# A graph-attention and slice-attention layer in float32: two orders of tokens for contiguous operands, two transposes moved to TensorE, denominators from a column of ones

## Chip, cores, metric

One core of a Trainium2 chip. The metric is the device time of one execution in microseconds (us), the median of several; all values quoted are of runs in the fast state. "Span" is the time from the first to the last record of the one profiled execution. A pass is one TensorE matmul instruction; a float32 matmul takes two (the views below have x32 for a run of 16 matmuls). The stationary operand of a matmul is the one that a weight load (LDWEIGHTS) puts in place, the moving operand is the other. In the views PE stands for the matmuls of TensorE, PEld for its weight loads, DVE for VectorE, ACT for ScalarE, POOL for GpSimd, SP for SyncE, and a `q` behind a name for the sequencer of that engine.

## The reference, cut to what matters

`x` is (32, 512, 256) float32: 32 batches of 512 tokens. Every batch goes through

```python
x = x + gnn(layernorm(x), adj, ...)     # mlp1 256->512, attention without mask, mlp2 512->256, attention with mask
x = x + ffn(layernorm(x), ...)          # softmax over 64 slices per head, sums per slice, attention among slices, back
# _gat: h = inp @ W; e = leaky_relu(f1_i + f2_j); att = softmax(e, axis=2); elu(att @ h)
# ffn:  w = softmax((x @ W_x @ W_slice) / temp); tok = (w^T x) W_fx / sum(w); attention; out = w @ out_slice
```

Each product needs one operand with features on the partitions and the other with tokens there, so every batch has several transposes.

## The kernel before

The kernel records all operations of the 32 batches and lets a list scheduler of its own merge them, so that three to four batches are in flight. The turns of the steps, a period and shifts for the first and last batches (`TURNS`, `PERIOD`, `HEAD`, `TAIL`) are constants found by a search and steer the order. Partition `p` of a tile of tokens holds tokens `4p..4p+3` (`NT` is 4), so a block of 128 tokens for one matmul is every fourth column of a feature-major tile:

```python
def every(cols, t):
    return cols[:, t::NT]
...
# h: the stationary operand (second argument) is strided
nc.tensor.matmul(pm, every(o0T[:, k], t), wfc[:, k, s, :], ...)
...
# transposes of the middle batches: VectorE turns 32x32 blocks, the DMA puts the blocks in place
def flip(src, dst):
    nc.vector.transpose(dst, src.rearrange("p (c i) -> p c i", i=Q))        # Q = 32
FLIPPED = ("xn", "u", "e", "o2", "w", "xn2", "s1")
flip(e, stage[:, :, i::NT]); ...; gather("e", stage, pT)     # 4 DMA writes to DRAM, 1 DMA back
...
# tokens: 16 small matmuls, 64 columns of stationary operand, s = 0 and 1 in the two halves of the array
for p in range(NP):
    for k in range(KD):
        for s in range(2):
            nc.tensor.matmul(pm[ts(s, C), p, :], wfx[:, k, ts(2 * p + s, C)],
                             every(s1T[:, k], p)[:, ts(s, G)], start=(p == 0 and k == 0), stop=False)
```

Of the kernel before, what the change touches and what calls it, by code (L numbers as in the profile page):

```python
# [15 lines left out]
TURNS = {  # L16
    "load": -28.1, "norm1": 42.5, "mlp1": 51.4, "h": 105.5, "factors": 105.5, "p": 114.2,
    "pv": 115.4, "o1": 126.5, "mlp2": 169.7, "h2": 183.7, "e": 190.4, "p2": 190.4,
    "pv2": 203.8, "norm2": 210.0, "w": 285.7, "sums": 288.2, "s1T": 298.5, "tokens": 342.3,
    "att": 351.0, "vo": 351.0, "gg": 361.3, "out": 377.9,  # L20
}
PERIOD, SPARE = 91.4, 0.00

HEAD, TAIL = (-48.2, -40.6, -1.9), (-3.9, 8.3, 26.1)


SAMPLE, SETUP = 8, 15.0

FLIPPED = ("xn", "u", "e", "o2", "w", "xn2", "s1")

P = 128
# [4 lines left out]
class Recorder:  # L36
# [4 lines left out]
    DRAIN = 0.17  # L41
    ISSUE, BEGIN, LAND, BEHIND = 0.45, 1.2, 0.9, 3.0
    KEPT = 1
# [62 lines left out]
    def _cost(self, op, out, ins):  # L106
# [6 lines left out]
        if op.method == "dma_start":  # L113
            side = next(ap for ap in (out, *ins) if ap.space != bass.MemoryType.DRAM)
            op.moving = out.size() * 4 / (250e3 if side.ap[0][1] <= P // 4 else 320e3)
            return self.ISSUE, 0.0
# [175 lines left out]
def adj_ffn_kernel(  # L292
# [71 lines left out]
    def gather(what, stage, dst):  # L364


        blocks, width = stage.shape[1:]
        scr = dram.tile([blocks, Q, P // Q, width], F32, name="scr", tag=f"scr_{what}", bufs=2)
        for a in range(P // Q):
            nc.sync.dma_start(  # L370
                scr[:, :, a, :].rearrange("c r j -> r c j"), stage[ts(a, Q), :, :]
            )
        nc.sync.dma_start(
            dst, scr.rearrange("(k c) r a j -> (c r) k (a j)", c=P // Q)
        )

    def every(cols, t):

        return cols[:, t::NT]

# [98 lines left out]
    adjt = new("adjt", [P, NT, N], tag="wT", dtype=I32)  # L479
    nc.sync.dma_start(adjt, adj.rearrange("(p t) j -> p t j", p=P))  # L480
    for t in range(NT):
        nc.vector.tensor_scalar(
            mbias[:, t, :].rearrange("p (t q) -> p t q", t=NT),
            adjt[:, t, :].rearrange("p (q t) -> p t q", t=NT), 0.0, None, op0=OP.is_gt,
        )
        nc.vector.tensor_scalar(
            mbias[:, t, :], mbias[:, t, :], -1.0, -MASKED, op0=OP.add, op1=OP.mult
        )
# [91 lines left out]

    def transpose_features(what, b, src, dst):

        if by_dma(what, b):
            stage = new(what + "_stage", [P, D // Q, P], tag="stage4")
            for t in range(NT):
                flip(src[:, t, :D], stage[:, :, t::NT])
            gather(what, stage, dst)
            return
        for k in range(KD):
            pt = tr_tile([P, N])  # L590
            for t in range(NT):
                nc.tensor.transpose(pt[:, ts(t)], src[:, t, ts(k)], ident)
            nc.scalar.copy(
                dst[:, k, :].rearrange("p (q t) -> p t q", t=NT),
                pt.rearrange("p (t q) -> p t q", t=NT),
            )

# [12 lines left out]
    def front(b):  # L610
# [7 lines left out]
        xnT = new("xnT", [P, KD, N])  # L618
        transpose_features("xn", b, xn, xnT)
        nc.step = "mlp1"  # L620
# [12 lines left out]
        for t in range(NT):  # L633
            for s in range(2):
                pm = mm_tile([P, HH + 1])
                for k in range(KH):
                    nc.tensor.matmul(
                        pm, every(o0T[:, k], t), wfc[:, k, s, :],
                        start=(k == 0), stop=(k == KH - 1),
                    )  # L640
                nc.scalar.copy(h[:, t, s, :], pm)
# [47 lines left out]
        for i in range(NT):  # L689
# [11 lines left out]
            if by_dma("u", b):  # L701
                flip(u, stage[:, :, i::NT])
                continue
            pt = tr_tile([P, KH, P])
            for m in range(KH):
                nc.tensor.transpose(pt[:, m, :], u[:, ts(m)], ident)
            nc.vector.tensor_tensor(o1T[:, :, i::NT], pt, o0T[:, :, i::NT], op=OP.add)
        nc.step = "o1"
        if by_dma("u", b):
            gather("u", stage, o1T)  # L710
            for m in range(KH):
                nc.vector.tensor_tensor(o1T[:, m, :], o1T[:, m, :], o0T[:, m, :], op=OP.add)
        return o1T

    def middle(b, o1T):
# [3 lines left out]
        for m in range(KD):  # L719
            pm = mm_tile([P, N])  # L720
            for k in range(KH):
                nc.tensor.matmul(
                    pm, w2[:, k, ts(m)], o1T[:, k, :], start=(k == 0), stop=(k == KH - 1)
                )
# [3 lines left out]
        for t in range(NT):  # L728
            pm = mm_tile([P, D + 2])
            for k in range(KD):  # L730
                nc.tensor.matmul(
                    pm, every(o2T[:, k], t), wh[:, k, :], start=(k == 0), stop=(k == KD - 1)
                )
# [8 lines left out]
        if by_dma("e", b):  # L742
            stage = new("e_stage", [P, N // Q, P], tag="stage")
        den = small("den", [P, NT])
        nmax = small("nmax", [P, NT])
        for i in range(NT):
# [7 lines left out]
            )  # L754
            nc.scalar.activation(
                e, e, AF.Exp, bias=nmax[:, i : i + 1], accum_out=den[:, i : i + 1]
            )
            if by_dma("e", b):
                flip(e, stage[:, :, i::NT])
                continue  # L760
            pt = tr_tile([P, NT, P])
            for j in range(NT):
                nc.tensor.transpose(pt[:, j, :], e[:, ts(j)], ident)
            nc.scalar.copy(pT[:, :, i::NT], pt)
        nc.step = "p2"
        if by_dma("e", b):
            gather("e", stage, pT)
        rd = small("rd2", [P, NT])
        nc.vector.reciprocal(rd, den)

        r2 = new("r2", [P, NT, D])
        if by_dma("o2", b):
            stage = new("o2_stage", [P, N // Q, KD * Q], tag="stage4")
            for k in range(KD):
                nc.vector.transpose(
                    stage[:, :, ts(k, Q)].rearrange("p (t c) i -> p t c i", t=NT),
                    o2T[:, k, :].rearrange("p (c i t) -> p t c i", t=NT, i=Q),
                )
            gather("o2", stage, r2)
        else:  # L780
            for t in range(NT):
                pt = tr_tile([P, D])
                for k in range(KD):
                    nc.tensor.transpose(pt[:, ts(k)], every(o2T[:, k], t), ident)
                nc.scalar.copy(
                    r2[:, t, :].rearrange("p (a k i) -> p k a i", k=KD, i=Q),
                    pt.rearrange("p (k a i) -> p k a i", k=KD, i=Q),
                )

# [3 lines left out]
        for i2 in range(NT // 2):  # L793
            pm = mm_tile([P, 2, D])
            for s in range(2):
                i = 2 * i2 + s
                for j in range(NT):
                    nc.tensor.matmul(
                        pm[:, s, :], every(pT[:, j], i), h[:, j, :D],
                        start=(j == 0), stop=(j == NT - 1),  # L800
                    )
            u, m = row("u2", (P, 2, D), "u"), row("m2", (P, 2, D), "m")
            elu_elu(
                [(pm[:, s, :], rd[:, 2 * i2 + s : 2 * i2 + s + 1], s) for s in range(2)], m, u
            )
            for s in range(2):
# [8 lines left out]
    def back(b, x1):  # L815
# [5 lines left out]
        xnT = new("xn2T", [P, KD, N])  # L821
        transpose_features("xn2", b, xn, xnT)

# [3 lines left out]
        if by_dma("w", b):  # L827
            stage = new("w_stage", [P, INNER // Q, P], tag="stage")
        for t in range(NT):
            pm = mm_tile([P, INNER])  # L830
            for k in range(KD):
                nc.tensor.matmul(
                    pm, every(xnT[:, k], t), weff[:, k, :], start=(k == 0), stop=(k == KD - 1)
                )
# [15 lines left out]
            if by_dma("w", b):  # L850
                flip(wt, stage[:, :, t::NT])
                continue
            pt = tr_tile([P, NP, P])
            for p in range(NP):
                nc.tensor.transpose(pt[:, p, :], w[:, t, ts(p)], ident)
            nc.scalar.copy(wT[:, :, t::NT], pt)
        if by_dma("w", b):
            gather("w", stage, wT)

# [5 lines left out]
        for p in range(NP):  # L865
# [9 lines left out]
            if by_dma("s1", b):  # L875
                flip(s1[:, p, :D], stage[:, :, p::NP])
        nc.step = "s1T"
# [3 lines left out]
        else:  # L881
            for k in range(KD):
                pt = tr_tile([P, INNER])
                for p in range(NP):
                    nc.tensor.transpose(pt[:, ts(p)], s1[:, p, ts(k)], ident)
                nc.scalar.copy(
                    s1T[:, k, :].rearrange("p (q n) -> p n q", n=NP),
                    pt.rearrange("p (n q) -> p n q", n=NP),
                )
# [13 lines left out]
        for p in range(NP):  # L903
            for k in range(KD):
                for s in range(2):
                    nc.tensor.matmul(
                        pm[ts(s, C), p, :], wfx[:, k, ts(2 * p + s, C)],
                        every(s1T[:, k], p)[:, ts(s, G)],
                        start=(p == 0 and k == 0), stop=False,
# [62 lines left out]
        for t2 in range(NT // 2):  # L972
            po = mm_tile([P, 2, D])
            for s in range(2):
                t = 2 * t2 + s
                for p in range(NP):
                    nc.tensor.matmul(
                        po[:, s, :], every(wT[:, p], t), gg[:, p, :],
                        start=(p == 0), stop=(p == NP - 1),
# [66 lines left out]
```

## Time and profile before

| | before |
|---|---|
| time, median | 2926 us |
| span of the profiled run | 2918.5 us |
| TensorE / VectorE / ScalarE busy | 97% / 76% / 36% |
| mean granted TensorE clock | 0.991 |
| first mm<-o1T,w of the 6th and of the 26th batch | 507.0, 2263.3 us |

The last row splits the run in three: filling up to the 6th batch (507 us), twenty steady batches (1756 us, 87.8 each) and emptying (655 us). In the views quoted below, a group's line is engine, operation, out<-in, shape and count; then busy time and mean ns of one; then the engine's idle time just before and what ended it. A timeline's line begins with start and duration in us.

### The profile page before, as it was taken

Reading aid. Unit: us, or ns where it says so; the run is one execution under the profiler, and the core shown is the slowest. Engines: PE = TensorE matmul, PEld = TensorE weight load, DVE = VectorE, ACT = ScalarE, POOL = GpSimd, SP = SyncE. Lnnn points to the kernel's source line nnn. Section 1 sums busy time; section 2 is a strip of 40 time slices with the busy share of each in tenths; the row PEclk is TensorE's granted clock in tenths of the full one; section 3 lists DMA queues with packets and bytes.
Section 4 is the critical chain, followed back from the end, with each engine's and each line's share of the span. In section 5 each row is a group of like instructions: output and inputs, shape, how many; then the busy total and the mean of one; then the engine's idle time right before and its main releaser. Section 6 shows DMA issues by size and latency. Waiting matters only on the chain.

```text
span 2918.5 us, 34260 instructions
## 1 busy us (share of the span) xinstructions
PE 2827.3 (97%) x11981; PEld 2301.0 (79%) x11981; DVE 2231.4 (76%) x4994; ACT 1042.8 (36%) x2058; POOL 125.2 (4%) x233
## 2 busy tenths in 40 slices
PE   8999899999999999999999999999999999999998
PEld 6787668887778887878887878887878877777776
DVE  6567768877778877778877778877778877788774
ACT  3533323333333333333333333333333333333232
POOL 0000000000000000000000000000000000000000
PEclk9999999999999999999999999999999999999998
DMA  5125345454445454445444445444445444444420
GB/s 163 31 72 143 96 128 152 129 147 131 134 139 151 127 148 129 135 135 157 123 145 130 137 137 156 126 144 130 138 137 153 129 140 129 136 138 116 137 73 15
DMA packets 459365, 373.24 MB, mean 128 GB/s; under 512 B 82229, under 2 KB 376761, under 8 KB 459065
## 3 DMA queue, kind: packets, MB, share of 16 engines
q1 hardware_dynamic: 455856, 368.92, 43.8%
q10 hardware_dynamic: 3336, 2.14, 0.2%
q8 instruction: 95, 1.56, 0.2%
q14 instruction: 78, 0.63, 0.1%
HBM read 196.91 MB, written 174.06 MB: 127 GB/s over the span
## 4 chain that ended last, share of the span: by engine, by line
PE 61%; DVE 21%; DMA 11%; SPq 3%; issue 2%; ACT 1%; DVEq 0%; ACTq 0%
PE mm L255 58%; DMA scr<-e_stage 5%; DVE e_stage L255 4%; SPq L255 3%; DMA o1T<-scr 3%; DVE e L255 3%; DVE w L255 3%; DVE w_stage L255 2%; PE tr L255 2%; DVE rs L255 2%; DVE nmax L255 2%; DMA scr<-u_stage 1%; PE sm L255 1%; DVE u L255 1%; DVE mx L255 1%
## 5 line engine op out<-in xcount | busy, mean ns | idle before, releaser
L255 PEld LDWEIGHTS mm<-wfc,o0T 128*128 128x128 f32 x2048 | 491.4, 327 | 19.3 <-PE tr L255 5.5
L255 PE MATMUL mm<-wfc,o0T 128*128 128x257 f32 x2048 | 498.7, 398 | 0.0
L255 PE MATMUL mm<-h,pT 128*128 128x256 f32 (+1 forms) x2048 | 486.8, 379 | 0.0
L255 PEld LDWEIGHTS mm<-h,pT 128*128 128x128 f32 x2048 | 390.2, 191 | 51.9 <-issue 2.8
L255 PE MATMUL mm<-xn,w 128*128 128x257 f32 x1024 | 272.8, 392 | 37.7 <-DVE fm L255 17.4
L255 PE MATMUL mm<-h,p2T 128*128 128x256 f32 x1024 | 301.3, 400 | 0.4 <-DMA p2T<-scr 0.4
L255 PEld LDWEIGHTS mm<-h,p2T 128*128 128x128 f32 x1024 | 266.7, 321 | 9.9 <-DMA p2T<-scr 0.7
L255 PE MATMUL mm<-xnT,w 128*128 128x512 f32 x512 | 258.6, 614 | 3.6 <-ACT xnT L255 3.3
L255 PE MATMUL mm<-gg,wT 128*128 128x256 f32 x1024 | 260.3, 401 | 0.0
L255 PEld LDWEIGHTS mm<-gg,wT 128*128 128x128 f32 x1024 | 251.5, 329 | 11.1 <-ACT gg L255 0.2
L255 PEld LDWEIGHTS mm<-xn,w 128*128 128x128 f32 x1024 | 186.6, 194 | 84.2 <-issue 50.6
L255 PE MATMUL mm<-weff,xn2T 128*128 128x512 f32 x512 | 243.6, 608 | 0.1
L255 ACT COPY h<-mm 128x257 f32<-128x257 f32 (+1 forms) x384 | 141.6, 369 | 279.6 <-PE mm L255 274.8
L255 PE MATMUL mm<-o1T,w 128*128 128x512 f32 x512 | 230.0, 602 | 9.6 <-DVE o1T L255 9.6
L255 DVE TENSOR_TENSOR o1T<-o1T,o0T 128x512 f32<-128x512 f32 x120 | 75.2, 687 | 157.6 <-DMA o1T<-scr 157.6
L255 PEld LDWEIGHTS mm<-o1T,w 128*128 128x128 f32 x512 | 96.0, 191 | 124.7 <-issue 91.6
L255 DVE SCALAR_TENSOR_TENSOR e<-f2b,h,mbias 128x512 f32<-128x512 f32 x128 | 92.4, 743 | 131.0 <-ACT f2b L255 129.0
L255 ACT ACTIVATE u<-mm,rd 128x256 f32<-128x256 f32 x192 | 90.0, 471 | 266.0 <-PE mm L255 159.1
L255 PEld LDWEIGHTS mm<-weff,xn2T 128*128 128x128 f32 x512 | 151.8, 315 | 40.2 <-ACT xn2T L255 1.3
L255 ACT ACTIVATE m<-m 128x512 f32<-128x512 f32 x192 | 118.0, 626 | 154.6 <-DVE m L255 154.1
L255 ACT ACTIVATE e<-e,nmax 128x512 f32<-128x512 f32 x128 | 92.4, 722 | 199.3 <-DVE nmax L255 199.3
L255 DVE STREAM_TRANSPOSE o_stage<-o2T 128x512 f32<-128x512 f32 x60 | 66.5, 1108 | 125.6 <-ACT o2T L255 123.9
(147 smaller groups left out, 4203.9 us busy)
## 6 DMA issues: line engine op xcount, KB each, us to landing
scr<-xn_stage SPq DMA_DIRECT2D x240, 128.0 KB, 2.6
scr<-u_stage SPq DMA_DIRECT2D x120, 256.0 KB, 4.5
o1T<-scr SPq DMA_DIRECT2D x30, 1024.0 KB, 6.1
scr<-e_stage SPq DMA_DIRECT2D x120, 256.0 KB, 4.9
p2T<-scr SPq DMA_DIRECT2D x30, 1024.0 KB, 5.6
scr<-w_stage SPq DMA_DIRECT2D x120, 256.0 KB, 4.1
wT<-scr SPq DMA_DIRECT2D x30, 1024.0 KB, 5.7
xt<-in_x_dram SPq DMA_DIRECT2D x32, 512.0 KB, 4.0
```

The lines of the kernel that those rows point to most:

```text
L255: getattr(getattr(self.nc, op.engine), op.method)(*op.args, **op.kwargs)
```

## The change

Intent: with `p = 32a+i`, let token `4p+t` stand at column `128a+32t+i` or at column `128t+p` in place of column `4p+t`, two orders in all, so that every stationary operand and every 32x32 transpose touches runs of 32 words or more; transpose the second layer norm (`xn2`) and the sums (`s1`) on TensorE; and get the softmax denominators of the second attention from a column of ones in `h2`. The scheduler's constants were searched anew; two costs in its model changed too, left out below (`BEHIND` 3.0 to 2.7, and the speed that it assumes for DMAs of 32 partitions, 250e3 to 215e3). The core of the diff, cut:

```diff
-TURNS = {"load": -28.1, "norm1": 42.5, ...}    PERIOD, SPARE = 91.4, 0.00
-HEAD, TAIL = (-48.2, -40.6, -1.9), (-3.9, 8.3, 26.1)
+TURNS = {"load": -84.2, "norm1": 231.3, ...}   PERIOD, SPARE = 94.3, 0.00
+HEAD, TAIL = (-18.3, -16.5, -8.8), (-4.0, -5.5, -4.1)
-FLIPPED = ("xn", "u", "e", "o2", "w", "xn2", "s1")
+FLIPPED = ("xn", "u", "e", "o2", "w")
-    def every(cols, t):
-        return cols[:, t::NT]
+    def swapped(cols):
+        return cols.rearrange("p (t a i) -> p a t i", t=NT, i=Q)
-                flip(e, stage[:, :, i::NT])                 # likewise xn, u, w
+                flip(e, stage[:, :, ts(i, Q)])
-                        pm, every(o0T[:, k], t), wfc[:, k, s, :],      # likewise o2T, p2T, wT, xn2T
+                        pm, o0T[:, k, ts(t)], wfc[:, k, s, :],
-            nc.scalar.activation(e, e, AF.Exp, bias=nmax[:, i : i + 1], accum_out=den[:, i : i + 1])
+            nc.scalar.activation(e, e, AF.Exp, bias=nmax[:, i : i + 1])
+        nc.vector.memset(h[:, :, D], 1.0)                   # and p2T @ h over D + 1 columns
+            raw = new("w_raw", [P, NP, N], tag="w")         # w comes back in the other order,
+            gather("w", stage_w, raw)                       # four ScalarE copies swap it into wT
-                        every(s1T[:, k], p)[:, ts(s, G)],   # moving operand of tokens
+                        s1T[:, k, :].rearrange("p (a n i) -> p n a i", n=NP, i=Q)[:, p, ts(s, 2)],
```

## The prediction

> **What bounds the kernel now.** I read the busy shares first, then the groups with shapes kept apart, then the timeline of TensorE in one steady batch, then the chain that ended last.
>
> ```profile
> PE 2827.3 (97%) x11981; PEld 2301.0 (79%) x11981; DVE 2231.4 (76%) x4994; ACT 1042.8 (36%) x2058; POOL 125.2 (4%) x233
> PE 61%; DVE 21%; DMA 11%; SPq 3%; issue 2%; ACT 1%; DVEq 0%; ACTq 0%
> ```
>
> TensorE is busy 97% of the span, so the time is what TensorE issues plus its waits. Successive batches start 87.6 us apart in the middle of the run (the first mm<-o1T,w of each batch); 32 x 87.6 = 2803, the rest of the 2918.5 us is filling and emptying the pipeline of batches. A matmul of float32 is two instructions (passes). Their mean durations overlap, so I take the pace from start times: gap to the next group over count.
>
> ```profile
> 1408.73 8.55 PE L255 MATMUL mm<-wfc,o0T 128*128 128x257 f32 x36
> 1417.11 0.67 PE L255 MATMUL mm<-xn,w 128*128 128x257 f32 x2
> ...
> 1443.35 10.55 PE L255 MATMUL mm<-h,pT 128*128 128x257 f32 x48
> 1453.74 0.27 PE L255 MATMUL sm<-ident,s 128*4 128x128 f32 x1
> 1453.94 2.07 PE L255 MATMUL mm<-s1T,wfx 128*64 128x64 f32 x32
> 1455.94 2.84 PE L255 MATMUL mm<-xnT,w 128*128 128x512 f32 x6
> ```
>
> A 257-column pass with a stationary operand taken at every fourth token costs (1417.11-1408.73)/36 = 233 ns; with one in one piece (1453.74-1443.35)/48 = 216.5 ns. The weight loads say why:
>
> ```profile
> L255 PEld LDWEIGHTS mm<-wfc,o0T 128*128 128x128 f32 x2048 | 491.4, 327 | 19.3 <-PE tr L255 5.5 <-issue 2.1
> L255 PEld LDWEIGHTS mm<-h,pT 128*128 128x128 f32 x2048 | 390.2, 191 | 51.9 <-issue 2.8 <-DVE pT L255 0.5
> ```
>
> 327 against 191 ns, most of it hidden under the running pass, so 136 ns more of load shows as only 16.5 ns. Under 512-column passes it is wholly hidden: ten strided mm<-weff,xn2T take 4.31 us, 431 ns each, and sixteen unstrided mm<-o1T,w 6.97 us, 436 each.
>
> **What the skill says.** (1) "SBUF — State Buffer", section "Door 1: The DMA port swizzle", has SBUF lines of 16 bytes with a penalty for each access in a new line. Four float32 are 16 bytes, the stride of this kernel, and the trace agrees: loads of 327 against 191 ns, and ScalarE copies out of PSUM of 1101 ns into a strided wT against 587 into f2b. (2) "TensorEngine Tiling (Array Packing)", "Key Properties": changing the tiling mode drains TensorE, and different tiles may load and multiply in parallel. The trace agrees on both: see the third part. (3) "VectorE: DVE Perf Modes", "The three transpose paths", tells only that VectorE transposes blocks of 32x32; the cost of a strided destination is not there. The trace has e_stage<-e at 1116 ns where other VectorE passes over 512 words take 660 to 690.
>
> **The change part by part.**
>
> *Strides.* Four groups of 256 to 258 columns get an unstrided stationary operand: wfc,o0T 2048 passes, h,p2T 1024, gg,wT 1024, wh,o2T 512; 4608 in all. 4608 x 16.5 ns = 76 us off TensorE. The 512 passes of weff,xn2T gain nothing.
>
> *Transposes onto TensorE.* In 30 batches 16 transposes are added (8 of xn2, 8 of s1); 16 of o2T at the two edge batches go: 464 more. Four tr<-ident,ex take 0.44 us, 110 ns each: 464 x 0.11 = +51 us on TensorE. In exchange VectorE loses 8 transposes of 0.64 us a batch, and the DMA queue two round trips.
>
> *Denominators.* h2 has a column of ones, so p2T passes have 257 columns instead of 256: under 1 us in all. ScalarE loses 128 accumulator reads (23.9 us), VectorE gets three small reciprocals and a memset a batch (0.5 us).
>
> *What only the order of the built kernel shows.* The tokens step (mm<-s1T,wfx, 64 columns of stationary, alternating between halves of the array) stood as one run of 16 matmuls in nearly every batch. In the changed kernel its 16 matmuls are strewn between mm<-h,pT: runs of 2, 4, 1, 1, 1, 1, 1, 1, 3, 1. Counted over the program, there are 263 such runs in place of 37. The filling phase of the kernel before happens to contain a few split runs:
>
> ```profile
> 394.42 0.70 PE L255 MATMUL mm<-h,pT 128*128 128x256 f32 x2
> 395.05 1.12 PE L255 MATMUL mm<-s1T,wfx 128*64 128x64 f32 x14
> 396.11 0.70 PE L255 MATMUL mm<-h,pT 128*128 128x256 f32 x2
> 396.74 1.12 PE L255 MATMUL mm<-s1T,wfx 128*64 128x64 f32 x14
> ...
> 2510.39 0.42 PE L255 MATMUL mm<-s1T,wfx 128*64 128x64 f32 x2
> 2510.74 0.65 PE L255 MATMUL mm<-nrow,bfx 4*64 4x256 f32 x4
> ```
>
> Two h,pT passes between two runs take 395.05-394.42 = 0.63 us instead of 0.43: +0.20 for going in (drain, about 0.09) and for the first full load after coming out, which nothing hides (about 0.10). A run of a single matmul takes 0.35 us by itself (2510.39 to 2510.74[...]), since its other half stands empty; an unbroken run of 16 takes 2.00 (1453.94 to 1455.94), 0.235 for each further pair. So a lone matmul costs 0.55 us. A steady batch: six lone ones 3.3; the 2 at 0.56; the 4 at 0.80; the 3 as two pairs 0.80; the last, which runs into nrow, 0.45; sum 5.9 us against 2.2 (2.00+0.20) before. That is +3.7 us a batch. Over the whole order, with the early and edge batches as they stand and a few nrow switches saved, I count +89 us.
>
> *Sum on TensorE:* -76 + 51 + 89 = **+64 us**. Added up instruction by instruction with these durations, the kernel before needs 2754 us, the changed one 2815: +61, which I use.
>
> *Waits.* The kernel before spends 2918 - 2754 = 164 us beyond that sum. The mean granted clock of 0.991 is 26 us of it, the start before the first matmul and the end after the last about 13, leaving some 125 for waits. About 1.5 us of each batch are waits of this kind:
>
> ```profile
> 1416.69 1.04 SPq L255
> 1417.77 4.65 DMA scr<-e_stage
> 1422.42 0.41 issue
> 1422.82 1.11 DVE w_stage L255
> ...
> 1426.70 0.67 PE mm L255 x2
> ```
>
> TensorE stands 0.68 us before that last line: w comes late, since VectorE was full with transposes and its w_stage buffer waited for the DMA of e_stage. The change takes much of this away: 5.1 us of VectorE's transposes a batch go, and the remaining 18 now write (o2: read) runs of 32 words. If those fall from 1.1 to 0.6 us (an estimate from the other 512-word passes; no trace shows it yet), and the halves likewise, that is another 8 us: VectorE from 69.9 to about 57 of 87.6. And a slower TensorE leaves everybody more slack. I take 65 of the 125 us back, mostly in the filling and emptying phases (14 us are lost between 350 and 439 alone) and the one wait a batch. Edge batches gain some from copies of 0.6 instead of 1.1 us.
>
> Predicted span: 2815 + 26 + 13 + 60 = 2914; the timed median lies 8 us above the traced span, so **2922 us**.
>
> **The rivals.** (A) *The strides decide.* If the split tokens cost nothing, for instance because the lone 64-column matmuls slip under h,pT, TensorE's sum is 2815-89 = 2726, and with the same 60 us of waits the time is about 2833, 3% faster. For it: this is the evident intent. Against it: the split runs quoted above. (B) *The waits stay or move.* The order is new; o1T<-scr and p2T<-scr have to land within about 20 and 28 us of TensorE work, near what they take now (21 us from the last h,pT to o1T), and wT now waits for the sums and four more ScalarE copies. If all 125 us stay, the time is 2815+26+13+125+8 = 2987, 2% slower. Against it: VectorE and the queue both get lighter and ScalarE is at 36%. (C) *DMA bound.* Unlikely, 128 GB/s and fewer transfers; worth nothing either way.
>
> **Range and chances.** Between A in part (half the cost of the split runs, waits at 50: 2870) and B in part (2975) I set 2880 to 2980. A gain over 2% needs less than 2868, where only 6 us of waits (2868-2815-26-13-8) would have room under my sum: 0.15. A loss over 2% needs over 2985, so all waits kept: 0.08. Within 2%: 0.77.
>
> **What would show it right or wrong.** In the changed profile: weight loads of wfc, p2T, gg and wh near 191 ns and passes at 216.5; transposes e_stage, u_stage, w_stage near 0.6 us; s1T,wfx runs of x2 between h,pT taking 0.35 us with the passes after them 0.2 longer than two h,pT passes need, some 5.9 us a batch; batches about 88.3 us apart; less idle of TensorE ahead of mm<-xn,w. Wrong would be: batches 85 us apart (then A), or TensorE idle over 2 us a batch ahead of o1T, p2T or gg (then B).

## The result, and the profile after

The changed kernel takes **2872.6 us** (2871.0 to 2874.2, 4 runs) against 2925.9: ratio 0.982, interval 0.980 to 0.984. Ratios here are the mean time of one kernel's fast runs over that of the other's of the same rounds, so not quite the ratio of the medians. It is 1.8% faster, within 2% but 7 us below the predicted range, 49 us below the predicted time.

| | before | after |
|---|---|---|
| span | 2918.5 | 2872.4 |
| mean granted clock | 0.991 | 0.996 |
| filling: first mm<-o1T,w of the 6th batch | 507.0 | 470.6 |
| twenty steady batches, each | 87.8 | 88.8 |
| emptying: from the 26th batch to the end | 655 | 625 |

So the steady batches became *slower* by 1 us, near the predicted 88.3 (by luck, see below), and the gain came all from filling and emptying, 66 us. The page of the changed kernel, busy shares and the chain that ended last by engine:

```profile
PE 2809.4 (98%) x12445; PEld 2056.7 (72%) x12445; DVE 2042.7 (71%) x4886; ACT 1137.3 (40%) x2162; POOL 128.5 (4%) x233
PE 87%; DMA 10%; SPq 1%; DVE 1%; ACT 1%; issue 0%; ACTq 0%; DVEq 0%
```

VectorE has left the chain (21% before, 1% now). The groups with shapes kept apart, two of the kernel before and then three of the changed one:

```profile
L255 PE MATMUL mm<-h,p2T 128*128 128x256 f32 x1024 | 301.3, 400 | 0.4 <-DMA p2T<-scr 0.4
L255 DVE STREAM_TRANSPOSE e_stage<-e 128x512 f32<-128x512 f32 x120 | 133.9, 1116 | 5.4 <-DMA scr<-w_stage 2.8 <-ACT e L255 2.4
```

```profile
L255 PEld LDWEIGHTS mm<-wfc,o0T 128*128 128x128 f32 x2048 | 385.7, 189 | 56.8 <-issue 1.2 <-PE tr L255 0.2
L255 PE MATMUL mm<-h,p2T 128*128 128x257 f32 x1024 | 244.0, 382 | 31.7 <-DMA p2T<-scr 31.6
L255 DVE STREAM_TRANSPOSE e_stage<-e 128x512 f32<-128x512 f32 x120 | 84.8, 707 | 57.0 <-ACT e L255 56.9
```

Weight loads take 189 instead of 327 ns, and the passes behind them run at 216 ns: eight of mm<-wfc,o0T take 337.54-335.81 = 1.73 us in the timeline of the filling below, so the 4608 x 16.5 ns are there. Transposes take 0.71 instead of 1.12 us. But TensorE now stands 31.6 us for p2T<-scr, a wait that the kernel before had for 0.4 us. The timeline of TensorE in the filling, and then in a steady batch at the split tokens and at that wait:

```profile
335.81 1.90 PE L255 MATMUL mm<-wfc,o0T 128*128 128x257 f32 x8
337.54 1.04 PE L255 MATMUL tr<-ident,s 128*128 128x128 f32 x8
338.41 0.27 PE L255 MATMUL sm<-ident,s 128*4 128x128 f32 x1
```

```profile
1501.74 0.70 PE L255 MATMUL mm<-h,pT 128*128 128x257 f32 x2
1502.37 0.45 PE L255 MATMUL mm<-s1T,wfx 128*64 128x64 f32 x8
1502.75 0.70 PE L255 MATMUL mm<-h,pT 128*128 128x257 f32 x2
1503.38 0.33 PE L255 MATMUL mm<-s1T,wfx 128*64 128x64 f32 x2
1503.64 2.00 PE L255 MATMUL mm<-h,pT 128*128 128x257 f32 x8
1505.57 0.33 PE L255 MATMUL mm<-s1T,wfx 128*64 128x64 f32 x2
...
1575.85 0.60 PE L255 MATMUL mm<-xn,w 128*128 128x257 f32 x2
1577.90 2.00 PE L255 MATMUL mm<-h,p2T 128*128 128x257 f32 x8 [1.46 <-DMA p2T<-scr]
```

Two h,pT passes between two runs take 1502.37-1501.74 = 0.63 us, exactly the +0.20 of the prediction. But a lone tokens matmul takes 1503.64-1503.38 = 0.26 us, not 0.35.

### The profile page after: what moved, and what is told of

It reads as the page before. It is cut to its first block, busy times and chain, and to the rows that moved or that the text cites. A ratio compares the mean times of both kernels' runs of the same rounds, so it can differ in the third digit from the quotient of the medians.

```text
span 2872.4 us, 34539 instructions
## 1 busy us (share of the span) xinstructions
PE 2809.4 (98%) x12445; PEld 2056.7 (72%) x12445; DVE 2042.7 (71%) x4886; ACT 1137.3 (40%) x2162; POOL 128.5 (4%) x233
## 4 chain that ended last, share of the span: by engine, by line
PE 87%; DMA 10%; SPq 1%; DVE 1%; ACT 1%; issue 0%; ACTq 0%; DVEq 0%
PE mm L255 81%; DMA p2T<-scr 7%; PE tr L255 4%; DMA scr<-e_stage 2%; SPq L255 1%; PE sm L255 1%; DMA wfc<-in_L_gnn_W_fc_dram 0%; ACT e L255 0%; DVE e_stage L255 0%; DMA xt<-in_x_dram 0%; DMA adjt<-in_adj_dram 0%; ACT s1T L255 0%; ACTq L255 0%; DVE tok L255 0%; ACT wT L255 0%
## 5 line engine op out<-in xcount | busy, mean ns | idle before, releaser
L255 PEld LDWEIGHTS mm<-wfc,o0T 128*128 128x128 f32 x2048 | 385.7, 189 | 56.8 <-issue 1.2
L255 PE MATMUL mm<-h,p2T 128*128 128x257 f32 x1024 | 244.0, 382 | 31.7 <-DMA p2T<-scr 31.6
L255 PE MATMUL mm<-gg,wT 128*128 128x256 f32 x1024 | 235.5, 379 | 0.0
L255 PEld LDWEIGHTS mm<-h,p2T 128*128 128x128 f32 x1024 | 183.5, 190 | 71.2 <-DMA p2T<-scr 39.4
L255 PEld LDWEIGHTS mm<-gg,wT 128*128 128x128 f32 x1024 | 193.4, 190 | 31.3 <-issue 4.3
L255 ACT ACTIVATE w<-w 128x512 f32<-128x512 f32 x128 | 80.5, 630 | 229.2 <-DVE w L255 228.9
L255 DVE SCALAR_TENSOR_TENSOR u<-m,u 128x512 f32<-128x512 f32 x192 | 131.4, 684 | 40.1 <-ACT m L255 37.5
L255 PEld LDWEIGHTS mm<-weff,xn2T 128*128 128x128 f32 x512 | 92.9, 190 | 73.4 <-issue 67.6
L255 PEld LDWEIGHTS mm<-xnT,w 128*128 128x128 f32 x512 | 91.0, 192 | 75.3 <-issue 69.0
L255 DVE RECIPROCAL rd<-mm 128x1 f32<-128x1 f32 x256 | 41.7, 163 | 138.5 <-PE mm L255 138.3
```

The source lines that it names most:

```text
L255: getattr(getattr(self.nc, op.engine), op.method)(*op.args, **op.kwargs)
```

## The experiments

All ratios of a step refer to the kernel before timed beside it (2920 to 2924 us). Differences to the changed kernel are to its 2872.6 us, from a session in which the kernel before took 2926 us, so they are good to about 5 us. "Same order" means that the order of instructions on every engine was compared with the parent kernel's and is identical; only access patterns or the place of one item differ. Where results are wrong on purpose, the run is a timing only.

### 1. Tokens in one run

```diff
+        # after scheduling: all 16 tokens matmuls of a batch are emitted where the last of them stood
```

> The changed kernel with the 16 tokens matmuls (mm<-s1T,wfx) of each batch kept as one run, at the place of the last of them; all else in the same order. Theory (each split run drains TensorE and leaves the other half of the array empty): 226 runs fewer, 89 us off TensorE's work, nothing between h2 and p2T touched, so the wait for p2T<-scr stays at about 1.3 us a batch: 2872 - 89 = about 2783 us (2765 to 2805), batches 85.4 us apart. Rival (the lone matmuls slip under mm<-h,pT, or another wait takes their place): 2855 to 2880 us.

2794.7 us, ratio 0.957: -78 us. The theory holds, the rival falls. The timeline of this kernel at the run:

```profile
1306.62 1.15 PE L267 MATMUL mm<-s1T,wfx 128*64 128x64 f32 x32
1307.70 0.64 PE L267 MATMUL mm<-nrow,bfx 4*64 4x256 f32 x2
```

One run of 16 takes 1.08 us, where the kernel before had 2.00. From the start times, tokens with their entries and exits cost 136 us in the changed kernel and 41 here, so 95 us went off TensorE and 78 off the time. Of the other 17 some became waits: the idle time of TensorE (span less busy) rose from 63 to 71 us.

### 2. The new wait: one load behind p2T<-scr instead of ahead of it

```diff
-  scr<-e_stage x4; x<-in_x_dram; p2T<-scr        # order on the DMA queue
+  scr<-e_stage x4; p2T<-scr; x<-in_x_dram
```

> The changed kernel, same order, except that the load of x for the second residual is issued after p2T<-scr instead of just before it. Theory: p2T<-scr lands in 6 to 6.5 us instead of 7.8, the wait of 1.35 us a batch goes to 0.2 or less: 2872 - 30 = 2842 us (2830 to 2855). Rival (the transfer's time is not from sharing): 2865 to 2880 us, landing still at 7.8.

2842.0 us, ratio 0.973: -31 us, and the wait is down to 1.1 us. The DMA issues of the changed kernel and of this one (KB, median us to landing):

```profile
p2T<-scr SPq DMA_DIRECT2D x30, 1024.0 KB, 7.8
```

```profile
p2T<-scr SPq DMA_DIRECT2D x30, 1024.0 KB, 5.9
```

The 512 KB issued just ahead held up the transfer that TensorE was about to need. The run shows that the place in the queue decides; that the two share the DMA engines is the explanation which the author gives for it.

### 3. Both

> The changed kernel with the tokens matmuls in one run (as in the run before) and the load of x for the second residual issued after p2T<-scr instead of just before it. Theory: 89 us off TensorE's work, and p2T<-scr, which shares the DMA engines with that load of 512 KB, lands about 1.3 us earlier, which takes most of the wait away: 2872 - 89 - 30 = about 2753 us (2735 to 2785), batches about 84.3 us apart. Rival (other waits take their place): 2800 us or more.

2761.5 us (2756.7 to 2764.5), ratio 0.945, correct results: 5.5% faster than the kernel before and the best of this study. Steady batches are 84.1 us apart. The two gains add (78 and 31 alone, 111 together).

### 4. Loads and transposes strided again in the changed kernel

```diff
-   nc.tensor.matmul(pm, o0T[:, k, ts(t)], ...)      # also o2T, p2T, wT     (loads)
+   nc.tensor.matmul(pm, o0T[:, k, t::NT], ...)
-   flip(e, stage[:, :, ts(i, Q)])                   # also xn, u, w, o2     (transposes)
+   flip(e, stage[:, :, i::NT])
```

> The changed kernel, same order, with the stationary operands of wfc,o0T, wh,o2T, h,p2T and gg,wT read at every fourth token again (results wrong on purpose). Theory: 4608 passes at 233 instead of 216.5 ns, +76 us of TensorE work; but 1.7 us of each batch's 2.4 lie between h2 and p2T, where the wait for p2T<-scr (1.3 us a batch) can swallow them, so +40 to +76: 2912 to 2948 us, weight loads near 327 ns, wait for p2T near zero. Rival (strides cost nothing on the path): within 10 us of 2872.

> The changed kernel, same order, with VectorE's 32x32 transposes of xn, u, e, w writing (o2: reading) every fourth word again (results wrong on purpose); 18 transposes a batch slow down from 0.7 to 1.1 us (xn 0.41 to 0.64), some 6.5 us of VectorE a batch. Theory (the faster transposes are a good part of what the filling and emptying and the waits gave back): batches 0.4 to 1.5 us farther apart, since e_stage is on the chain to p2T, and a longer filling: 2885 to 2925 us. Rival (VectorE has slack everywhere): within 8 us of 2872.

> The changed kernel, same order, with both undone: transposes that touch every fourth word and strided stationary operands (results wrong on purpose). Each alone gave 2937 and 2926 us. Theory (the strided loads fill the time in which TensorE waits for p2T, so the two overlap): 2960 to 2985 us. Rival (they add up): 2991 us or more.

Loads: 2936.6 us (+64; runs of 2929 to 2949), and the wait for p2T<-scr fell from 31.6 to 6.5 us: it swallowed 25 us, as foretold. Transposes: 2926.3 us (+54), 1 us above the range expected. That wait grew to 53.4, by 22 us, and the clock was halved more often (mean 0.989 against 0.996), which is another 20. Both: 2952.9 us (+80), less than the lower edge of what was expected. With both, 15.6 us of that wait are left and the clock is at 0.997, so part of what the transposes alone cost is not there. What is swallowed depends on what waits: neither part has one price.

### 5. The same two parts alone in the kernel before, same order

```diff
-   nc.tensor.matmul(pm, every(o0T[:, k], t), ...)
+   nc.tensor.matmul(pm, o0T[:, k, ts(t)], ...)
-   flip(e, stage[:, :, i::NT])
+   flip(e, stage[:, :, ts(i, Q)])
```

> The kernel before, same order on every engine, with its 32x32 transposes writing (o2: reading) runs of 32 words instead of every fourth word (results wrong on purpose): 1.1 us each becomes 0.7, 8 us of VectorE a batch. Theory (late w and o1T are waits on VectorE, and they also stop TensorE long enough in the filling to lower its clock): the waits of some 1.5 us a batch mostly go, and the first five batches get 10 us or more shorter: 2865 to 2890 us. Rival (VectorE has slack): within 10 us of 2922.

> The kernel before, same order, with the stationary operands of wfc,o0T, wh,o2T, h,p2T and gg,wT in one piece (results wrong on purpose). TensorE's work falls by 76 us (4608 passes, 16.5 ns). Theory (TensorE sets the pace but VectorE's late w is close behind it): a part is swallowed by longer waits for w and o1T: 2860 to 2895 us. Rival A (nothing swallowed): 2846 us. Rival B (VectorE sets the pace): 2910 us or more.

> The kernel before, same order, with both: transposes that touch runs of 32 words and stationary operands in one piece (results wrong on purpose). Theory (the two add up and a little more, since fast transposes take away the wait that would swallow the loads' gain): 2790 to 2825 us, 50 to 80 us below the changed kernel, whose split tokens and transposes on TensorE cost 89 and 51 us. Rival (they swallow each other): 2850 us or more.

Transposes alone: 2863.9 us (-56, 1 us below the range; the first five batches got 8 us shorter, 507.0 to 498.8, where 10 or more were expected). Loads alone: 2889.5 us (-31, of 76 us taken off TensorE). Both: 2797.2 us (-123), more than the sum of 87. Who waited for whom, TensorE only, in the kernel before and then with the loads alone (us in total, times, longest):

```profile
PE mm L255 <- DVE fm L255: 17.4, 23, 1.1
PE mm L255 <- DVE o1T L255: 9.6, 13, 1.3
PE mm L255 <- DVE w L255: 9.5, 8, 4.1
```

```profile
PE mm L255 <- DVE fm L255: 28.0, 23, 1.7
PE mm L255 <- DVE o1T L255: 20.4, 23, 1.9
PE mm L255 <- DVE w L255: 19.5, 34, 4.1
```

The three waits on VectorE grew from 36.5 to 67.9 us: it was close behind TensorE, and a faster TensorE ran into it. With the transposes fast too they are mostly gone. So VectorE, at 76%, held up a TensorE at 97%.

### 6. The moving operand of tokens

```diff
   # changed kernel, strided again                          # kernel before, in one piece
-  s1T[...rearrange(...)][:, p, ts(s, 2)]                   -  every(s1T[:, k], p)[:, ts(s, G)]
+  s1T[:, k, p::NP][:, ts(s, G)]                            +  s1T[:, k, ts(p)][:, ts(s, G)]
```

> The changed kernel, same order, with only the moving operand of the tokens matmuls (s1T) read at every fourth word again (results wrong on purpose). In the changed profile a lone tokens matmul takes 258 ns and in the kernel before 352, a whole run of 16 takes 1082 (tokens in one run) against 2003. Theory (the moving operand of a 64-column pass is what got faster, and the prediction's split runs were sized with the slow one): lone runs at 352 ns again, TensorE's tokens 28 us longer over the program: 2893 to 2905 us, with 5 us either way for waits. Rival (the runs are faster for another reason, such as what stands around them): 258 ns still, within 6 us of 2872.

> The kernel before, same order, with only the moving operand of the tokens matmuls read in runs of words (results wrong on purpose). Theory: the run of 16 falls from 2.00 to 1.08 us, 29 us over the program, part of which may turn into waits: 2890 to 2905 us. Rival: 2.00 us still and within 6 us of 2921.

> The kernel before, same order, with everything that the layout makes contiguous at once: the transposes, the four stationary operands and the tokens' moving operand (results wrong on purpose). Without the last it took 2797 us. Theory: another 15 to 29 us less: 2768 to 2782 us, which is some 95 us below the changed kernel: what the layout is worth without the new order and the transposes on TensorE. Rival: 2790 us or more, swallowed by waits.

Strided again in the changed kernel: 2924.5 us. Its timeline:

```profile
1523.45 0.42 PE L255 MATMUL mm<-s1T,wfx 128*64 128x64 f32 x2
1523.80 2.00 PE L255 MATMUL mm<-h,pT 128*128 128x257 f32 x8
```

A lone matmul is back at 0.35 us, so it is the operand, not the neighbourhood; the rival falls. Tokens take 36 us longer on TensorE. The other 16 us of the +52 were not expected: in this run the clock was halved more often (mean 0.989 against 0.996, some 22 us), partly offset by a shorter wait for p2T<-scr (26.2 against 31.6 us). In the kernel before, in one piece: 2913.2 us, only -7, a miss of the expectation. The run of 16 fell to 1.24 us, 22 us over the program, but the waits for o1T grew from 9.6 to 17.5 us and others with them: the same swallowing as in 5. Everything contiguous at once in the kernel before: 2771.0 us, ratio 0.949, as expected. (The check of results passed the two runs of tokens alone although they read the wrong columns of s1T, so it does not see an error of this kind.)

### 7. Runs that the scheduler reordered

Six runs changed constants or a step of the recorded program, so that the scheduler made a new order: the constants of the other kernel, each way; the transposes of xn2 or of s1 by DMA again (with tokens in one run); those two transposes on TensorE in the kernel before; and the shifts `HEAD`, `TAIL` of the changed kernel in the kernel before.

> The changed kernel with the scheduler constants (turns of the steps, period, shifts at head and tail) of the kernel before. Theory (the layout and the faster transposes shorten filling and emptying, the constants only choose the order; the old constants keep tokens in one run): TensorE's work about 89 us less where tokens stay whole, some new waits: 2790 to 2860 us. Rival (the new constants are what made filling and emptying short): 2870 us or more, with the first five batches as long as in the kernel before.

> The kernel before with the scheduler constants of the changed kernel. Theory (constants alone don't help: strided loads, slow transposes and DMA round trips stay, and tokens may be split): 2920 to 3000 us, filling no shorter than before. Rival (the constants are what made filling and emptying short): the first five batches 30 us shorter than in the kernel before, as in the changed one.

> The changed kernel with tokens in one run (2795 us) and, in addition, xn2 transposed on VectorE and by DMA again; the scheduler orders anew. TensorE's work falls by 30 x 8 x 0.109 = 26 us. Theory (the short path of xn2 is part of what shortens filling and emptying): the first five and the last six batches take 10 us or more longer than with tokens in one run alone, which gives back a third or more: 2780 to 2810 us. Rival (TensorE's work alone decides): 2768 us, filling and emptying as before.

> The changed kernel with tokens in one run (2795 us) and, in addition, s1 transposed on VectorE and by DMA again; the scheduler orders anew. TensorE's work falls by 26 us. Theory (short path of s1 shortens filling and emptying): the first five and last six batches 10 us or more longer, 2780 to 2810 us. Rival (TensorE's work alone): 2768 us.

> The kernel before with the transposes of xn2 and s1 on TensorE and nothing else of the change; the scheduler orders anew with its own constants, and tokens fall into runs of 7 and 9. TensorE's work grows by 52 us of transposes and some 12 of the second run a batch. Theory (8 fewer transposes of 0.64 us and two shorter paths take waits and filling away): steady batches at 87.5 to 89.5 us, the first five batches 10 to 35 us shorter than in the kernel before, 2900 to 2960 us. Rival (the work on TensorE is simply added): 2985 us.

> The kernel before with only the shifts of the first and last batches (HEAD, TAIL) of the changed kernel. Theory (what shortens filling is the work and the paths, not these shifts): within 15 us of 2922, the first five batches within 10 us of 507. Rival (the shifts make the filling short): the first five batches 25 us or more shorter, 2890 us.

Measured: 3343.8, 3945.0, 3521.2, 6221.8, 3330.9 and 3004.6 us. None of the expectations held, theory or rival, except that 3343.8 lies in the open range of one rival (2870 us or more), 470 us above its edge. In all six the order that came out is bad, for example with s1 by DMA, TensorE waits (us, times, longest):

```profile
PE mm L267 <- DMA p2T<-scr: 579.4, 30, 24.3
PE mm L267 <- DVE o1T L267: 305.6, 29, 11.7
```

The shifts `HEAD` and `TAIL` alone, up to 30 us each, moved the filling from 507 to 580 us. The exchanged constants did not include the two costs of the model (`BEHIND` and the DMA speed), so even the runs of "the other kernel's constants" are not its scheduler. These runs tell nothing about the price of a part; they tell that the order can be worth hundreds of microseconds. (One more, with both transposes by DMA in the changed kernel, could not be scheduled at all.) This is why experiments 1 to 6 leave the order alone. It also means that the transposes on TensorE and the denominators could not be tested by themselves.

## Why the prediction was wrong, point by point

**What held.** Loads at 189 ns and passes at 216; the 16 transposes a batch at 0.109 us (eight of tr<-ident,s from 337.54 to 338.41); the split runs and their entry and exit of 0.20 us; VectorE as the cause of the waits (experiment 5) and its relief, though a smaller one (transposes of 0.71 us where 0.6 was said, VectorE busy 64 us of a steady batch where 57 was); a gain of less than 2%. Rival B came true in small: the new wait for p2T<-scr, 1.3 us a batch.

**What held by luck.** Steady batches came at 88.8 us where 88.3 was said, but two errors cancel in it. From the start times the tokens of a steady batch take 4.8 us, entries and exits included (2.8 of their own and ten times 0.20) where the prediction had 5.9. And TensorE's idle time did not go away there: it rose from 1.0 to 1.3 us a batch, the old waits of mm<-xn,w gone and the one for p2T<-scr come in their place. So by place the whole miss lies in filling and emptying: the prediction leaves 2914 - 20 x 88.3 = 1148 us for them, and they took 1096.

**Which step failed: the size of the split tokens (+89 us).** The step took every duration of a tokens matmul from the kernel before: 0.35 us alone, 0.235 for each further pair. There its *moving* operand was strided, and the prediction counted only stationary operands and transposes as strided ("Four groups ... get an unstrided stationary operand"). The same change puts the moving operand into runs of 32 words. With that a lone matmul takes 0.26 us and the whole term, own time plus entries and exits from the start times, is 136 - 73 = +63 us instead of +89. That is 26 us of the miss, 28 by the author's count, which leaves out what the 89 counts as saved on changes of tile in front of mm<-nrow,bfx. Experiment 6 shows the cause: with the moving operand strided the lone matmul is back at 0.35, and the kernel takes 2924.5 us.

**The rest of the 49 us.** The clock: the prediction carried 26 us of loss over unchanged; in the changed kernel the clock was halved for 24 us, a loss of 12, so 14 us less. The 8 us between span and timed median, a difference of one profiled run, did not recur (2872.4 and 2872.6). 28 + 14 + 8 = 50. What is left for waits is then 2872.4 - (2815 - 28) - 12 - 13 = 60 us, as predicted, but this is a remainder of the author's count of TensorE's work (2754 and 2815 us), which no view shows. The idle time in the pages (span less busy) fell from 91 to 63 us, by 28 and not by 65, and 31.6 of the 63 are a wait that the prediction did not foresee. (The ends of matmuls are modelled, so very short waits do not show as idle time.) So the size of the waits is not shown to have been right. Two readings of the prediction are also a little off: the views have 12 us of idle time between 350 and 439, not 14, and 1.0 us in a steady batch, not 1.5.

Where the clock was lost, before: among other places behind a wait for w in the filling. These are the end of that wait and the stretch from 361 to 370 us of the kernel before; the columns of the second view are busy us by engine (instructions), then PEclk, DMA share and GB/s:

```profile
359.46 1.06 PE L255 MATMUL mm<-xn,w 128*128 128x257 f32 x2 [4.08 <-DVE w L255]
```

```profile
361.00:370.00 9.00, 5.82 (x12) 3.32 (x13) 8.38 (x18) 2.46 (x5) 0.00 (x0) 0.51 0.49 117
```

TensorE stood 4.1 us for w until 359.5, and by the clock records it had half its clock from 359.6 for 10.2 us; from 361 to 370 it was busy 5.8 of 9 us while VectorE was busy 8.4. "TensorE: Matmul & The Clock Gate", section "What's actually happening", says that a monitor of activity halves the clock by windows of 3413 ns; the records agree, the halved stretches of the two kernels are 3.4, 6.8 or 10.2 us long, but for the last one of each, which the end cuts off. So here a wait cost more than its own length. The changed kernel has no such wait at that place. But the faster transposes alone did not remove it: with them, in the old order, TensorE stood nearly as long,

```profile
354.79 1.20 PE L255 MATMUL mm<-xn,w 128*128 128x257 f32 x2 [3.49 <-DVE w L255]
```

and the clock was halved for 13.7 us from 354.3. With fast transposes, or with everything contiguous, the old order stays at a mean clock of 0.992. So the 14 us that the clock gave back came with the rest of the change, and whether the transposes on TensorE or the new order did it is open.

**Where the time went, in all.** The contiguous access patterns, everything else left as it was, are worth 149 us (2920 to 2771). This is not the whole layout, since the four ScalarE copies a batch that bring w into the other order are not in that run. Transposes on TensorE, these copies, the new order and the rest of the change gave some 102 back (2771 to 2872.6). Of that, the split tokens cost 78 (experiment 1) and the load ahead of p2T<-scr 31 (experiment 2); mending both gives 2761.5, 10 below the 2771. So the transposes on TensorE, 51 us of its work by count, seem about paid for by shorter filling and fewer waits. This is argued and not shown: the balance also holds the new order, the copies and the denominators, and no run separates them.

**What stays open.** Filling fell by 36 us. With everything contiguous in the old order it falls by 21.5 (485.5 against 507.0); the other 15 belong to the rest of the change, the transposes on TensorE and the new order among it. Emptying fell by 30, and by 32 with the contiguous patterns alone (623), so there these are enough. Why the clock was halved in many steady batches with strided tokens and with strided transposes but not in the changed kernel is not settled. They lie in two different places: with strided tokens they begin some 30 us after the wait for p2T<-scr, behind the split runs, and with strided transposes nearly all begin within 1.3 us of the end of that wait.

## What to carry to other kernels

When an access pattern changes, list every operand that it touches, moving ones too, and take durations for the prediction only from rows with the same pattern; and read the built order, since a scheduler that prices a small matmul by its columns (0.06 us in `_cost` here, where a lone one takes 0.26 and its entry and exit 0.20) will strew it where it costs more. An engine at 76% can hold up one at 97%: taking work off the busier one alone gave 31 of 76 us here, relieving both 123. In a kernel whose order is searched, test a part with the order frozen, and look at the DMA queue just ahead of the transfer that ends a wait.

## What the Trainium skill lacked or had wrong

- "SBUF — State Buffer", "Door 1: The DMA port swizzle", has the 16-byte lines, and the runs agree for weight loads (327 to 189 ns), VectorE transposes (1116 to 707 ns) and ScalarE copies (wT<-tr, 1101 to 587 ns). It has no size for TensorE and does not name its moving operand, which pays as well: a lone tokens matmul of two 64-column passes took 0.35 us strided by 16 bytes and 0.26 in runs of 32 words, a run of 16 took 2.00 and 1.08.
- "TensorE: Matmul & The Clock Gate", "LDWEIGHTS (loading the stationary operand)", has a load time by columns but none for a strided operand, nor how much of it shows: 136 ns more of load cost 16.5 ns of a 257-column float32 pass and nothing of a 512-column one.
- "TensorEngine Tiling (Array Packing)", "Key Properties", names the drain at a change of mode without a size: here the last mm<-h,pT pass before a run of 64-column tokens took about 0.09 us longer, start to start, and the first one behind it 0.10.
- "VectorE: DVE Perf Modes", "The three transpose paths", has no cost of a strided destination: 128x512 float32 took 1.12 us written at every fourth word and 0.71 in runs of 32 words.
- No page that was read has a figure for what a load issued just ahead on the same queue costs a waited-for transfer: 1 MB landed in 7.8 us behind a load of 512 KB and in 5.9 ahead of it.
